# Batch 1's statistics ahead of the filters and mixing matrices, and raw matrices through two buffers

## The chip, the cores and the metric

The kernel runs on one core of a Trainium2 chip. The metric is the device time of one execution in microseconds (us), median of several executions. The engines are PE (matmul), DVE (vector), ACT (scalar), POOL (GpSimd) and SP (SyncE, which here only issues DMAs).

## What is computed

Two layers over an input of 2 batches x 128 channels x 64 x 64 positions, so 4096 tokens of 128 values a batch.

```python
x = conv_attention(x)                 # group norm, 4-head attention with rotary positions, residual
t = to_tokens(x)                      # (2, 4096, 128)
n = layernorm(t)
t = t + softmax(n @ n.T) @ n          # attention of the second layer, no projections
u = layernorm(t)
# four branches i on the first T / 2**i tokens; y_hard picks one of them
#   U+, U- = causal convolutions of u (and of u with alternating signs) with 16 filters phi
#   s_i = sum_k sigma_k**0.25 * (U+_k @ Mphi_plus[i, k] + U-_k @ Mphi_minus[i, k]) + 3 taps with M_u[i]
t = t + sum_i weight_i * pad(s_i)
```

The parts that matter here: the layer norm of the tokens ahead of the second layer's attention (batch 1's above all), and the 16 mixing matrices, which are the weighted sums over the four branches of `M_phi_plus[:, k]` and `M_phi_minus[:, k]`, times sigma_k to the power 0.25, stored as their sum and their difference.

## The kernel before

The program has four stages: the first layer's attention for both batches (up to about 1030 us), the second layer's attention for batch 0 and then for batch 1 (`attend`, up to about 1850 us), and the filter stage (the rest). All of it is unrolled Python that issues instructions one after the other. The framework then orders each engine's instructions: an instruction that is ready sooner may go ahead of one that was issued earlier, among ready ones the earlier issued goes first, and buffers of one tag are handed on as they come free. `tc.keep_in_program_order` pins an instruction behind the instruction that was issued just before it on its engine. It is used on the first `bn_stats` of each four (L692) and on the normalisation (L708).

`attend(b, p, beside, ...)` (L876) treats the 4096 x 4096 scores in quarters of 512 tokens: for j in 0 to 7, i from j to 7, so 36 blocks (j, i), since the scores are symmetric. In each block PE makes the scores (L890), ACT their exponentials (L899), PE transposes them (L906), ACT and DVE split the transposed ones into two parts (L908, L909), DVE splits the untransposed ones (L947, L948), and PE multiplies both with the tokens (L916). `close(j)` (L924) divides and adds to the tokens, with transposes on PE at L935, and calls `closed(j)`. PSUM banks for transposes come from `bank(...)`, two buffers of one tag for all users.

Other work runs beside the attention as a generator, `beside`: `next(beside, None)` is called twice a block between the scores (L975) and twice around the sums (L978, L979); in the first block only the first two are. What is left when the blocks are done is run to its end (L983).

For batch 0, `beside` is the chain in L1084:

1. `left`: what the first layer still has to do (one division and the projection of the last quarter, L333 to L364). It completes the tokens of batch 1.
2. `filters` (L792): loads phi, four small matmuls, copies into a table tile `tb`, two stores.
3. `matrices` (L846): branch weights, the tap matrices `mu`, the coefficients, and then for each of 16 k: two loads into the tile `raw` (L865, L866: 128 x 4 x 2 x 128 floats, 512 KB), a step of the generator, a weighted sum over the four branches on DVE (L716, L718), sum and difference written back into `raw` (L871, L872), and a store to `mx` in DRAM (L873). `raw` has a single buffer, so load k + 1 waits for store k.
4. `normalise(1, ...)` (L742): the statistics of batch 1 (`LayerStats.steps`, L699: eight steps of four `bn_stats` L690 and `bn_aggr` L693, and the reciprocal root, L88 on DVE and L89 on POOL), then for each quarter i the normalised tokens `y` (L709), their split into `hi` and `lo`, their transposes through a bank (L757), and the split of those (L758, L761). Quarter i waits until `closed(i)` has been called, since it overwrites what batch 0's attention reads.

The tag `raw` is also used by `tb` and `mu_raw`. The tag `low` (one buffer) holds batch 0's low parts on their way from DRAM: `ready(i)` (L1066) loads and casts quarter i + 1 at the start of block (0, i), so the last of them is asked for at block (0, 6). The stored matrices `mx` are first read in the second attention (L1097), the filter tables in the filter stage.

Of the kernel before, what the change touches and what calls it, by code (L numbers as in the profile page):

```python
# [12 lines left out]
F32 = mybir.dt.float32  # L13
# [9 lines left out]
P = 128  # L23
B, C, HH, WW = 2, 128, 64, 64
# [10 lines left out]
NK = 16  # L35
NU = 3
NBR = 4
# [26 lines left out]
def conv_attn_hybrid(ctx: ExitStack, tc: tile.TileContext, io):  # L64
    nc = tc.nc
# [25 lines left out]
    def pool(stack, name, bufs=1, **kw):  # L91
        return stack.enter_context(tc.tile_pool(name=name, bufs=bufs, reuse_waits="tile", **kw))
# [5 lines left out]
    def chain(*parts):  # L98
        for p in parts:
            yield from p  # L100
# [613 lines left out]
    def weighted_sum(dst, src, w):  # L714

        nc.vector.tensor_scalar(dst, src[:, 0], w[:, 0:1], None, ALU.mult)  # L716
        for i in range(1, NBR):
            nc.vector.scalar_tensor_tensor(dst, src[:, i], w[:, i : i + 1], dst, ALU.mult, ALU.add)  # L718
# [5 lines left out]
    def layers(st, layer0):  # L724
# [3 lines left out]
        tok = [tokens[b].tile([P, NI, C], F32, tag="t", name=f"tok{b}") for b in range(B)]  # L728
        px = pool(st, "px", side="right")
        right0, right1 = (st.enter_context(ExitStack()) for _ in range(2))  # L730
        last = pool(right0, "last", 2, side="right")
# [6 lines left out]
        def first_parts():  # L738
            hiT.append(px.tile([P, L], F32R, tag="a", name="hiT"))
            hi.append(Columns([px.tile([P, HALF], F32R, tag=f"b{n}", name=f"hi{n}") for n in range(2)]))  # L740

        def normalise(b, p, stage, gate=None):  # L742

            stats = LayerStats(p, tok[b], f"a{b}")
            yield from stats.steps()
            for i in range(NQ):
                while gate is not None and gate[0] <= i:
                    yield
                cols = bass.ts(i, 512)
                y = stage(i, 0)  # L750
                for t in range(4):
                    stats.normed(y[:, bass.ts(t, P)], 4 * i + t)
                nc.vector.tensor_copy(hi[0][:, cols], y)
                yield
                pt = side[0](f"yT{b}_{i}")
                for t in range(4):
                    nc.tensor.transpose(pt[:, bass.ts(t, P)], y[:, bass.ts(t, P)], ident)  # L757
                nc.vector.tensor_copy(hiT[0][:, cols], pt)  # L758
                low = (stage(i, 1), stage(i, 0)) if b == 0 else (loT[0][:, cols], lo[0][:, cols])
                for n, (src, first) in enumerate(((pt, hiT[0][:, cols]), (y, hi[0][:, cols]))):  # L760
                    nc.vector.tensor_tensor(low[n], src, first, ALU.subtract)  # L761
                    if b == 0:
                        nc.sync.dma_start(lows[i, n], low[n])
                yield

        def beside_last(stage):
            first_parts()
            stages = [stage(n) for n in range(2)]
            yield from normalise(0, last, lambda i, n: stages[n][:, i])


        left = layer0(tok, px, last, side, beside_last)
        psum, bank = banks(psum_a)
        side[0] = bank
# [7 lines left out]
        def transform(p):  # L782

            fw = p.tile([P, 4, NF], F32, name="fw", bufs=1)
            nc.sync.dma_start(fw, io["fw"])
            return fw
# [5 lines left out]
        def filters(p, fw):  # L792
            phi = p.tile([P, 2, TROW], F32, tag="phi", name="phi")
            nc.sync.dma_start(phi, io["phi"])
            yield
            for s in range(2):
                tb = p.tile([P, 2, 2 * TROW], F32, tag="raw", name=f"tb{s}")
                tbr = tb.rearrange("w i (o c k) -> w i c o k", c=2, k=NK)
                for c in range(2):
                    ph = bank(f"ph{s}_{c}")[:, :TROW]  # L800
                    nc.tensor.matmul(ph, fw[:, c, :], phi[:, s, :], start=True, stop=True)
                    ph = ph.rearrange("w (o k) -> w o k", k=NK)
                    nc.vector.tensor_copy(tbr[:, 0, c], ph)
                    if c == 0:
                        nc.vector.tensor_copy(tbr[:, 1, 1], ph)
                    else:
                        nc.vector.tensor_scalar(tbr[:, 1, 0], ph, -1.0, None, ALU.mult)
                    yield
                nc.sync.dma_start(tables[:, s], tb)
# [36 lines left out]
        def matrices(p):  # L846
            wbr = branch_weights(p)
            mu_raw = p.tile([P, NBR, NU, C], F32, tag="raw", name="mu_raw")
            nc.scalar.dma_start(mu_raw, io["mu"].rearrange("i n d e -> d i n e"))
            weighted_sum(mu, mu_raw, wbr)  # L850
            nc.sync.dma_start(gw, io["gw"])
            nc.vector.tensor_tensor(gw, gw, mask.unsqueeze(1).to_broadcast([P, 2, P]), ALU.mult)

            sig = p.tile([P, NK], F32, name="sig")
            nc.gpsimd.dma_start(sig, io["sigma"].partition_broadcast(P))
            quarter = p.tile([P, NK], F32, name="quarter")
            nc.gpsimd.memset(quarter, 0.25)
            nc.gpsimd.tensor_tensor(sig, sig, quarter, ALU.pow)
            coef = p.tile([P, NK, NBR], F32, name="coef")
            for k in range(NK):  # L860
                nc.vector.tensor_scalar(coef[:, k, :], wbr, sig[:, k : k + 1], None, ALU.mult)
            yield
            for k in range(NK):
                raw = p.tile([P, NBR, 2, C], F32, tag="raw", name=f"raw{k}")
                nc.sync.dma_start(raw[:, :, 0, :], io["mpp"][:, k].rearrange("i d e -> d i e"))  # L865
                nc.sync.dma_start(raw[:, :, 1, :], io["mpm"][:, k].rearrange("i d e -> d i e"))  # L866
                yield
                pm = p.tile([P, 2, C], F32, tag="pm", name=f"pm{k}")
                weighted_sum(pm, raw, coef[:, k, :])
                own = raw[:, 0]  # L870
                nc.vector.tensor_tensor(own[:, 0, :], pm[:, 0, :], pm[:, 1, :], ALU.add)  # L871
                nc.vector.tensor_tensor(own[:, 1, :], pm[:, 0, :], pm[:, 1, :], ALU.subtract)  # L872
                nc.sync.dma_start(mx[k], own)  # L873
                yield

        def attend(b, p, beside, closed, ready=lambda i: None):  # L876
# [181 lines left out]
        with ExitStack() as l1:  # L1058
            p1 = pool(l1, "l1")
            lo.append(p1.tile([P, L], F32R, name="lo"))  # L1060
            fw = transform(p1)
            with ExitStack() as part:
                p = pool(part, "l1_a")
                gate = [0]

                def ready(i):  # L1066
                    for n in range(2) if i == 0 else [i + 1]:
                        if n < NQ:
                            low = p.tile([P, 2, 512], F32, tag="low", name=f"low{n}")
                            nc.sync.dma_start(low, lows[n].rearrange("n p c -> p n c"))  # L1070
                            nc.vector.tensor_copy(loT[0][:, bass.ts(n, 512)], low[:, 0])
                            nc.vector.tensor_copy(lo[0][:, bass.ts(n, 512)], low[:, 1])

                def closed(j):
                    gate[0] = j + 1

                y = [None]

                def stage(i, n):
                    y[0] = p.tile([P, 512], F32, tag="y", name=f"y1_{i}")  # L1080
                    return y[0]

                steps = normalise(1, p1, stage, gate)
                attend(0, p1, chain(left, filters(p, fw), matrices(p), steps), closed, ready)  # L1084
            right0.close()

            mxr, mxl = (x[0].rearrange("p (k s c) -> p k s c", k=NK, s=2) for x in (hiT, loT))
            with ExitStack() as part:
                p = pool(part, "l1_b", 2)
                fed = LayerStats(ffw, tok[1], "f1")  # L1090

                def closed(j):
                    fed.take(range(4 * j, 4 * j + 4))
                    fed.close(range(4 * j, 4 * j + 4))
                    own = slice(2 * j, 2 * j + 2)
                    m = p.tile([P, 2, 2, C], F32, tag="m", name=f"m{j}")
                    nc.sync.dma_start(m, mx[own].rearrange("k p s c -> p k s c"))  # L1097
                    nc.vector.tensor_copy(mxr[:, own], m)
                    nc.vector.tensor_tensor(mxl[:, own], m, mxr[:, own], ALU.subtract)

                attend(1, p1, feed(0, p, bank, fw), closed)
# [165 lines left out]
        fw = transform(late_pool)  # L1267
        beside = chain([None] * WC, feed(1, late_pool, one_bank, fw, fed))
        steps = 0
# [153 lines left out]
```

## Time and profile before

| | us |
|---|---|
| median of 3 runs (2992.15 to 2994.43) | 2992.23 |
| the profiled execution | 2991.11 |
| its span in the profile | 2989.3 |
| PE busy, of the span | 2862.9 (96%) |
| DVE busy | 1738.8 (58%) |
| ACT busy | 1835.8 (61%) |
| POOL busy | 665.1 (22%) |

Times in the profile count from the start of the span. A line of the timeline has start, duration, engine, line of the source, operation, written tile <- read tiles, shape, count, and in brackets the idle time before it with what ended it. "SPq" is SyncE's queue issuing a DMA. Durations of consecutive DVE instructions overlap a little, so starts tell more than sums. A matmul of 512 columns shows 0.39 us but starts every 0.23 us.

### The profile page before, as it was taken

The page shows a single profiled execution, that of the slowest core. Times are in us where ns is not written, and L with a number is a line of the kernel's source. Part 1 is how long each engine was busy: PE and PEld are TensorE (multiplying, and loading weights), DVE is VectorE, ACT ScalarE, POOL GpSimd, SP SyncE. Part 2 cuts the span into 40 slices and gives each one's busy share as a digit, 9 for nine tenths or more (in the row PEclk, how much of TensorE's full clock was granted, in tenths as well). Part 3 has the DMA queues.
Part 4 walks back from the last instruction along what each step waited for, and adds up shares of the span by engine and source line. Part 5 has one row for each costly group of instructions (what it writes and reads, how often), then busy time and mean ns, then how long its engine had stood idle before and what let it go on. Part 6 is the DMA issues. An engine that isn't in the chain of part 4 may idle for free. (4 is left out here: it accounts for less than half of the span.)

```text
span 2989.3 us, 40111 instructions
## 1 busy us (share of the span) xinstructions
PE 2862.9 (96%) x13872; PEld 1822.1 (61%) x13872; DVE 1738.8 (58%) x3060; ACT 1835.8 (61%) x2363; POOL 665.1 (22%) x1328
## 2 busy tenths in 40 slices
PE   5999999999999999399999999999999999999997
PEld 2555555555455578288677786666666666666665
DVE  5364662364252389578866777555555555556553
ACT  4999999999999844144444454444444444444542
POOL 4031130021000000100101102433444444444440
PEclk9999999999999999699999999999999999999999
DMA  5021120021010132200011001333343334333331
GB/s 147 26 82 48 54 70 4 20 71 38 5 43 24 39 99 65 62 1 1 15 36 44 12 22 50 91 96 100 83 87 84 83 79 114 80 84 82 81 83 49
DMA packets 165777, 175.91 MB, mean 59 GB/s; under 512 B 45264, under 2 KB 109536, under 8 KB 165568
## 3 DMA queue, kind: packets, MB, share of 16 engines
q1 hardware_dynamic: 121760, 136.00, 16.4%
q0 software_dynamic: 40816, 34.04, 5.4%
q10 hardware_dynamic: 2992, 3.22, 0.3%
q8 instruction: 115, 1.88, 0.3%
q14 instruction: 94, 0.77, 0.1%
HBM read 130.68 MB, written 25.49 MB: 52 GB/s over the span
## 5 line engine op out<-in xcount | busy, mean ns | idle before, releaser
L433 ACT ACTIVATE e<-s 128x1536 f16<-128x1536 f32 (+1 forms) x704 | 936.7, 1428 | 35.9 <-PE s L190 31.0
L1174 DVE TENSOR_TENSOR xl<-cv,xh 128x1024 fp32r<-128x1024 f32 x512 | 603.0, 1219 | 436.5 <-ACT xh L1173 350.0
L1173 ACT CAST xh<-cv 128x1024 fp32r<-128x1024 f32 x512 | 494.7, 1018 | 523.6 <-PE cv L1164 511.8
L1139 POOL DMA_DIRECT2D tokens_in<-rows x1024 | 490.5, 487 | 680.5 <-PE cv L1164 577.1
L190 PE MATMUL s<-qs,ks 128*128 128x512 f16 x2048 | 557.5, 379 | 8.5 <-ACT e L433 3.4
L190 PE MATMUL acc<-e,v 128*97 128x512 f16 x2048 | 557.3, 379 | 3.4 <-DVE accs L389 0.2
L1196 PE MATMUL m<-xh,loT 128*128 128x512 f32 x1024 | 409.8, 400 | 0.0
L1196 PE MATMUL m<-xh,hiT 128*128 128x512 f32 x1024 | 403.2, 394 | 0.0
L190 PEld LDWEIGHTS <-v 128*97 128x97 bf16 x2048 | 254.6, 124 | 214.5 <-issue 12.5
L899 ACT ACTIVATE ey<-y,nshift 128x512 f32<-128x512 f32 x288 | 196.1, 690 | 302.1 <-PE y L890 214.8
L190 PEld LDWEIGHTS <-ks 128*128 128x128 f16 x2048 | 200.5, 99 | 227.6 <-issue 42.3
L1164 PE MATMUL cv<-tables_in,tokens_in 32*128 32x512 f32 x2048 | 300.0, 645 | 1.4 <-DVE xl L1174 1.2
L1196 PE MATMUL m<-xl,hiT 128*128 128x512 f32 x1024 | 292.3, 417 | 1.2 <-DVE xl L1174 0.5
L1196 PEld LDWEIGHTS m<-xl,hiT 128*128 128x128 f32 x1024 | 178.8, 189 | 175.8 <-issue 104.7
L1196 PEld LDWEIGHTS m<-xh,loT 128*128 128x128 f32 x1024 | 192.7, 188 | 90.7 <-issue 47.8
L1196 PEld LDWEIGHTS m<-xh,hiT 128*128 128x128 f32 x1024 | 192.4, 188 | 42.2
L916 PE MATMUL oacc<-ep,hi 128*128 128x512 f32 x576 | 209.4, 410 | 2.7 <-DVE ep L948 1.8
L909 DVE TENSOR_TENSOR eT<-eT,eT 128x512 fp32r<-128x512 f32 x224 | 146.0, 684 | 109.4 <-ACT eT L908 108.9
L389 DVE COPY accs<-acc 97x512 f32<-97x512 f32 x64 | 44.2, 690 | 275.2 <-PE acc L190 275.1
L948 DVE TENSOR_TENSOR ep<-ey,ep 128x512 fp32r<-128x512 f32 x288 | 191.9, 683 | 5.4 <-PE oacc L916 0.4
L908 ACT ACTIVATE eT<-eT 128x512 fp32r<-128x512 f32 x224 | 133.0, 607 | 94.6 <-PE eT L906 93.9
L916 PE MATMUL oacc<-eT,hi 128*128 128x512 f32 x448 | 155.7, 409 | 3.3 <-DVE oT L956 2.3
(191 smaller groups left out, 3024.0 us busy)
## 6 DMA issues: line engine op xcount, KB each, us to landing
tables_in<-tables SPq DMA_DIRECT2D x1024, 64.0 KB, 3.4
tab<-in_rot SPq DMA_DIRECT2D x32, 512.0 KB, 4.1
tokens_in<-rows POOLq DMA_DIRECT2D x1024, 16.0 KB, 3.2
qs<-term POOLq DMA_DIRECT2D x128, 64.0 KB, 2.2
rows<-uh SPq DMA_DIRECT2D x64, 128.0 KB, 1.9
ks<-term POOLq DMA_DIRECT2D x96, 64.0 KB, 1.9
accs<-back SPq DMA_DIRECT2D x32, 128.0 KB, 2.3
lows<-stage SPq DMA_DIRECT2D x16, 256.0 KB, 2.0
```

Source lines behind the costliest of these rows:

```text
L190: tc.keep_in_program_order(nc.tensor.matmul(*args, **kw))
L433: nc.scalar.activation(e[:, own, :], ps[:, own, :], AF.Exp, scale=SCORE_SCALE)
L899: nc.scalar.activation(e[:, 2 * h + q, :], ps[:, q, :], AF.Exp, bias=nshift, accum_out=den[:, t, i : i + 1])
L908: nc.scalar.activation(eT[0], pt, AF.Copy, accum_out=den[:, 4 * i + u, j : j + 1])
L909: nc.vector.tensor_tensor(eT[1], pt, eT[0], ALU.subtract)
L916: nc.tensor.matmul(acc, a[0][:, own], c, start=(start and t == 0 and n == 0), stop=(stop and t == len(es) - 1 and n == 2),)
L948: nc.vector.tensor_tensor(es[t][1], e[:, t, :], es[t][0], ALU.subtract)
L1139: nc.gpsimd.dma_start(ut[part, :, :], rows[b][ci, row : row + BP, w0 : w0 + WC // 2, :])
L1164: nc.tensor.matmul(pu[:, h, :], ut[grp, w % 2, :], tt[grp, w % 2, :], start=True, stop=True)
L1173: nc.scalar.copy(hi, pu.rearrange("d h (c k) -> d k h c", k=NK))
L1174: nc.vector.tensor_tensor(seconds[n % 2][:, :, w, 64 * g2 : 64 * g2 + 64].rearrange("d k (h c) -> d k h c", h=2), pu.rearrange("d h (c k) ...
L1196: nc.tensor.matmul(acc, m, x, start=(s == 0 and w == 0 and i == 0), stop=(s == 1 and w == WC - 1 and i == len(products) - 1),)
```

## The change

Three edits. The statistics object of batch 1 is made outside `normalise` and its steps run right behind `left`, ahead of the filters and the matrices. The raw matrices alternate between the tags `raw` (even k) and `low` (odd k, free by then). And loads 0 and 1 are issued together before the first matrix, and load k + 2 one step after matrix k is stored. For batch 0 the same statistics are made at the same place as before, only written out at the call.

```diff
-        def normalise(b, p, stage, gate=None):
-
-            stats = LayerStats(p, tok[b], f"a{b}")
-            yield from stats.steps()
+        def normalise(b, stats, stage, gate=None):
+
+
             for i in range(NQ):
...
             stages = [stage(n) for n in range(2)]
-            yield from normalise(0, last, lambda i, n: stages[n][:, i])
+            stats = LayerStats(last, tok[0], "a0")
+            yield from stats.steps()
+            yield from normalise(0, stats, lambda i, n: stages[n][:, i])
...
             yield
+            raws = {}
+
+            def load(k):
+                if k < NK:
+                    raws[k] = p.tile([P, NBR, 2, C], F32, tag="low" if k % 2 else "raw", name=f"raw{k}")
+                    nc.sync.dma_start(raws[k][:, :, 0, :], io["mpp"][:, k].rearrange("i d e -> d i e"))
+                    nc.sync.dma_start(raws[k][:, :, 1, :], io["mpm"][:, k].rearrange("i d e -> d i e"))
+
+            load(0)
+            load(1)
+            yield
             for k in range(NK):
-                raw = p.tile([P, NBR, 2, C], F32, tag="raw", name=f"raw{k}")
-                nc.sync.dma_start(raw[:, :, 0, :], io["mpp"][:, k].rearrange("i d e -> d i e"))
-                nc.sync.dma_start(raw[:, :, 1, :], io["mpm"][:, k].rearrange("i d e -> d i e"))
-                yield
+                raw = raws[k]
                 pm = p.tile([P, 2, C], F32, tag="pm", name=f"pm{k}")
                 weighted_sum(pm, raw, coef[:, k, :])
                 own = raw[:, 0]
                 nc.vector.tensor_tensor(own[:, 0, :], pm[:, 0, :], pm[:, 1, :], ALU.add)
                 nc.vector.tensor_tensor(own[:, 1, :], pm[:, 0, :], pm[:, 1, :], ALU.subtract)
                 nc.sync.dma_start(mx[k], own)
+                yield
+                load(k + 2)
                 yield
...
-                steps = normalise(1, p1, stage, gate)
-                attend(0, p1, chain(left, filters(p, fw), matrices(p), steps), closed, ready)
+                stats = LayerStats(p1, tok[1], "a1")
+                steps = chain(left, stats.steps(), filters(p, fw), matrices(p), normalise(1, stats, stage, gate))
+                attend(0, p1, steps, closed, ready)
```

## The prediction

> **What bounds the kernel now.** I read the page's 40 slices first, for a hole in the busiest engine.
>
> ```profile
> PE   5999999999999999399999999999999999999997
> DVE  5364662364252389578866777555555555556553
> PEclk9999999999999999699999999999999999999999
> ```
>
> PE is full everywhere but in slice 17 (74.7 us each, so about 1195 to 1270 us), and there the granted clock drops too. The busy time by stretch then places the hole (columns: length, PE, PE loads, DVE, ACT, POOL, each with its count, clock, DMA share, GB/s).
>
> ```profile
> 1036.00:1208.00 172.00, 169.64 (x822) 136.08 (x822) 153.78 (x351) 81.95 (x248) 3.02 (x2) 0.98 0.27 84
> 1208.00:1264.00 56.00, 6.98 (x23) 4.23 (x24) 29.04 (x124) 0.69 (x2) 8.29 (x9) 0.52 0.22 67
> 1280.00:1300.00 20.00, 20.00 (x104) 16.49 (x103) 13.49 (x27) 9.27 (x29) 0.00 (x0) 1.00 0.01 2
> ```
>
> From 1036 to 1208 us PE is 98.6% busy and DVE 89%. From 1208 to 1264 PE issues 23 matmuls, and half of DVE is idle. In the clean attention stretch (third line) DVE needs only 67%. PE's waits and its own timeline name the culprit.
>
> ```profile
> PE yT L757 <- DVE lmva L693: 47.9, 2, 40.4
> ```
>
> ```profile
> 1207.58 0.40 PE L890 MATMUL y<-hiT,loT 128*128 128x512 f32 x1
> 1248.42 0.45 PE L757 MATMUL yT<-ident,y 128*128 128x128 f32 x1 [40.45 <-DVE lmva L693]
> 1248.66 0.63 PE L935 MATMUL o<-ident,fin 128*128 128x128 f32 x2
> ```
>
> PE stands at the transpose of batch 1's first normalised quarter (L757), which needs y, which needs the statistics. Attention work (L935, whose input was ready at 1196) queues behind it. Now DVE's timeline in that hole:
>
> ```profile
> 1212.52 0.28 DVE L872 TENSOR_TENSOR raw<-pm 128x128 f32<-128x128 f32 x1
> 1218.44 0.35 DVE L716 TENSOR_SCALAR pm<-raw,coef 128x256 f32<-128x256 f32 x1 [5.63 <-DMA raw<-in_mpm]
> ...
> 1245.01 0.28 DVE L872 TENSOR_TENSOR raw<-pm 128x128 f32<-128x128 f32 x1
> 1245.21 0.48 DVE L690 BATCH_NORM_STATS2 lsta<-tok 128x6 f32<-128x128 f32 x2
> ```
>
> DVE works off the last five mixing matrices, waiting 5.6 us for each load, and starts the statistics 0.2 us after the last of them. SyncE's queue shows why each load is late: one buffer.
>
> ```profile
> 1212.83 0.34 SPq L873 DMA_DIRECT2D mx<-raw  x1
> 1214.56 0.37 SPq L865 DMA_DIRECT2D raw<-in_mpp  x1
> 1214.97 0.51 SPq L866 DMA_DIRECT2D raw<-in_mpm  x1
> 1220.90 0.34 SPq L873 DMA_DIRECT2D mx<-raw  x1
> ```
>
> Store, 1.73 us until it has landed, load, 3.9 us until DVE may start (1214.56 to 1218.44), 2.4 us of DVE: 8.1 us for each k, all in series. While attention runs beside it, DVE's part takes some 4 us instead and a turn is about 10 us (issues at 1128.5, 1138.1, 1147.7).
>
> **What the skill says.** "PSUM — Partial Sum Buffer", section "Engine vs sequencer instructions": the Vector queue is strictly first in, first out and matmuls start in program order. The trace agrees: ready transposes (L935) stood 40.4 us behind L757. "DMA: Bandwidth & Descriptors", section "Two DMAs through the same engine are not ordered": only the completion semaphore orders them, so the issuer waits for it. That is the 1.73 us from store to load. The same page's "Rules for kernel authors" says to issue a load early and wait late; the 5.6 us waits are what happens otherwise. "TensorE: Matmul & The Clock Gate", Part 1: the array's clock halves when idle and comes back after about 3.4 us busy. Here the clock was 0.52 in the hole.
>
> **Order in the code.** One step of the side generator is taken four times in each block (j, i) of the attention, twice in the first. The rest of `left` takes 11 steps: the last division 7 (its wait is 5), the projection 4. Before: filters begin at step 12, matrix k is computed at step 19 + 2k, so the last at step 49, statistics at step 50, first y at step 59. Block n holds steps 4n - 1 to 4n + 2, so steps 49 and 50 are the last two of block 12 and only matmuls lie between them: the statistics, pinned behind DVE's previous instruction, are pinned behind the last matrix. After: statistics at steps 12 to 19, filters from 21, loads 0 and 1 at 27, matrix k at 28 + 2k (the last at 58), first y at 60. Between 58 and 60 lie L909's of block 15, so y is pinned behind attention work and not behind a matrix.
>
> **The change part by part**
>
> Statistics moved. 32 L690, 32 L693, 8 L88 on DVE. The first four tiles ran from 1245.21 to about 1246.8, 1.56 us, so 8 x 1.56 = 12.5 us if alone; mixed with other work a pair advanced DVE by about 0.28 us (two L690 at 1249.89 free the engine at 1250.27, then L693 takes 0.08), hence 32 x 0.28 + 0.5 = 9.5 us. They now fall into blocks 3 to 5, about 1082 to 1105 us. Eight POOL powers (L89, 1.0 us each) move past POOL's small loads and its power of sigma, which in the trace ran at 1030 to 1038. If those queue behind them, the coefficients come at about 1105 instead, still before the first matrix: nothing. POOL was busy 3.0 of 172 us, which is the cover.
>
> Filters moved. The same instructions 9 steps later, 2.25 blocks of about 11 us, 24 us. In the trace the chain from the first filter copy (1068.3) to the first matrix (1100.8) is 32 us of copies, two table stores, and the mu load. The first matrix should so come at about 1125, block 7, where its step is. Nothing on PE reads the tables or matrices before the second attention, past 1450 us: no cost.
>
> Two buffers. Issues stay 32 loads and 16 stores on SyncE's queue. Load k + 2 still waits for store k (1.7 us), with store k + 1 and load k + 3 queued behind it; two chains of about 10 us alternate, so 5 us for each k, 16 in 80 us, done at about 1205 to 1210 if DVE keeps up. Load 1 waits for the last `low` quarter to be cast (1089.5 in the trace; its load is traced at block 6, load 1 at block 7), so it waits for nothing then. Two loads together moved at 512 KB in 3.9 us, under 5: DMA isn't the bound.
>
> The stall removed. 56.0 us from 1208 to 1264 hold 21 transposes (0.13 us each at full rate: eight take 1.04) and 2 products (0.23): 3.2 us. So 52.8 us to gain.
>
> What is late next: DVE. Before block 15 it must now do what lay in the hole: statistics 9.5 and five matrices. A matrix mixed with attention takes DVE 1.9 us (1142.17 to 1145.89 less what lies between: 0.26 + 3 x 0.40 + 2 x 0.20), alone 2.4. So 9.5 + 9.5 = 19.0 us, at most 12.5 + 12 = 24.5, into 172 - 153.8 = 18.2 us of idle. Of that idle 12.0 was waits of attention work for ACT or PE (the waits to 1208: 6.5, 3.7, 1.8), which ready side work can fill, or not. Excess: 0.8 us with all filled, 24.5 - 6.2 = 18.3 us at worst; below nothing is excluded, as DVE work is only added there. In a block of 10.2 us (L954 from 1150.57 to 1160.73) attention needs 0.67 x 10.2 = 6.8 and two matrices 3.7: 10.5, just over. I take 5 us. After block 15 DVE is at 67 to 82%, so nothing is left behind.
>
> Normalising quarters 0 and 1 lay in the hole too, about 3.2 us of DVE each. In the open, PE waits for little of it: 0 to 3 us, I take 1.
>
> Sum against the profiled execution: 2991.1 us (span 2989.3 and 1.8 around it) - 52.8 + 5 + 1 = 2944.3. The median shown is 1.1 above that execution: **2945 us**.
>
> **Rivals**
> - DVE becomes the bound (15%). For: it was 98% busy from 1190 to 1208. Against: PE lost nothing there. With the worst sums, 18.3 + 3, and up to 10 us of y waiting behind matrices in the DVE queue: about 2962.
> - The change doesn't do what it says, and the stall stays (7%): y is queued behind the last matrix all the same and a turn takes 7.5 us, as loads and DVE get in each other's way. Then that matrix ends at 1125 + 16 x 7.5 = 1245 as now, and only PE's second wait (7.45, the rest of the 47.9) and a little of the slow clock go, some 10 us: 2982. Against: y is no longer pinned to a matrix, and 512 KB take 3.9 us.
> - Slower (3%). DVE's order assumes a matrix landed sooner than it lands, and each of 16 holds DVE, with attention behind it, for the whole 3.9 us from issue: 62 us lost for 52.8 gained, with the 5 us above 3006. It decides from a mean wait of (52.8 - 6)/16 = 2.9 us. Against: up to 1208 L716 waited 1.4 us in all, for 11 matrices with one buffer.
> - More than hoped (5%): no DVE excess and the attention's own small waits (PE lost 2.4 us to 1208) go too: 2936.
>
> **Numbers.** Forecast case (2937 to 2957) 70%, the others as given. The range, 2937 to 2965, holds the first and two thirds of the DVE case: 80%. Within 0.2% (6 us, about what can be told from no change) I put 2 of the stall rival's 7%: faster 95, same 2, slower 3.
>
> **What will show it.** Right: no wait of PE for lmva; L690 at about 1082 to 1105; matrix loads in overlapping pairs, starting at about 1125 and 5 us apart; DVE over 95% in blocks 7 to 14; the clock unbroken. Wrong: L757 again with a wait of tens of us, or waits of L716 for raw above 2 us each while attention runs.

## The result and the profile after

The median is 2946.4 us (2943.7 to 2948.6, four executions) against 2992.2 before (2988.7 to 2994.4, four). The ratio is 0.985, with a 95% interval of 0.983 to 0.987: 45.8 us less, or 1.5%. The forecast was 2945 in a range of 2937 to 2965. The profiled execution took 2948.6 us, with a span of 2946.7.

First the slices of the changed kernel (73.7 us each).

```profile
PE   5999999999999999999999999999999999999997
DVE  5264563265243289878866777555555555556553
PEclk9999999999999999999999999999999999999999
```

The hole in slice 17 is closed, and the clock is unbroken. By stretch (length, PE, PE loads, DVE, ACT, POOL, clock, DMA share, GB/s):

```profile
1208.00:1264.00 56.00, 54.20 (x277) 43.83 (x276) 45.59 (x96) 25.84 (x80) 0.00 (x0) 1.00 0.04 13
1125.00:1225.00 100.00, 91.42 (x442) 69.80 (x441) 95.42 (x234) 43.30 (x129) 0.10 (x1) 1.00 0.35 105
```

Where PE had issued 23 matmuls it now issues 277. The second line is the price: while the matrices run, DVE is 95% busy and PE 91%. PE's waits from 1028 to 1470 us (total, times, longest):

```profile
PE y L901 <- DVE loT L1082: 5.7, 1, 5.7
PE eT L917 <- DVE eT L920: 3.3, 6, 1.2
PE oacc L927 <- DVE ep L959: 3.2, 9, 0.6
...
PE yT L756 <- DVE y L709: 0.3, 1, 0.3
```

The 47.9 us for the statistics (`lmva` holds the means and variances) are gone; the transposes of y (now L756) wait 0.3 us. The first line is no new wait: it stands at 1041, where PE waits for the low parts of batch 0's first tokens (`loT`), and the kernel before had it too:

```profile
PE y L890 <- DVE loT L1071: 5.5, 1, 5.5
```

New are the small waits for DVE's part of attention in the other lines. DVE's own timeline where y is made:

```profile
1198.27 0.35 DVE L716 TENSOR_SCALAR pm<-raw,coef 128x256 f32<-128x256 f32 x1
1198.66 0.69 DVE L920 TENSOR_TENSOR eT<-eT,eT 128x512 fp32r<-128x512 f32 x1
1199.26 0.47 DVE L718 SCALAR_TENSOR_TENSOR pm<-raw,coef,pm 128x256 f32<-128x256 f32 x1
1199.66 0.34 DVE L709 TENSOR_SCALAR y<-tok,lmva,lrsa 128x128 f32<-128x128 f32 x1
...
1201.22 0.28 DVE L880 TENSOR_TENSOR raw<-pm 128x128 f32<-128x128 f32 x1
```

y (L709) goes between the instructions of a matrix, and one more matrix follows later. Nothing holds it behind the last one. SyncE's queue shows two interleaved chains:

```profile
1156.92 0.34 SPq L882 DMA_DIRECT2D mx<-raw  x1
1158.82 0.37 SPq L869 DMA_DIRECT2D raw<-in_mpp  x1
...
1162.41 0.34 SPq L882 DMA_DIRECT2D mx<-raw  x1
1164.13 0.37 SPq L869 DMA_DIRECT2D raw<-in_mpp  x1
...
1167.00 0.34 SPq L882 DMA_DIRECT2D mx<-raw  x1
```

A store still precedes the load into its buffer by 1.7 to 1.9 us, but stores now come 5 us apart instead of 8 to 10.

One caution on comparing traces. The first layer, which no kernel here touches, ended at different times in the profiled executions (the table's first column). So I compare the stage: from the load of fw, which opens the second layer, to the first store of transformed tokens (rows<-uh), which is in the second attention. Before, then after:

```profile
1028.75 0.35 SPq L785 DMA_DIRECT2D fw<-in_fw  x1
...
1473.98 0.36 SPq L1022 DMA_DIRECT2D rows<-uh  x1
```

```profile
1032.97 0.35 SPq L786 DMA_DIRECT2D fw<-in_fw  x1
...
1430.73 0.36 SPq L1033 DMA_DIRECT2D rows<-uh  x1
```

445.2 us became 397.8: 47.4 us less. That is all of the difference; the spans differ by 42.6, as the second layer began 4.2 us later in this trace. From there to the first filter matmul it is 359.3 us in both, and from that to the end 1156.0 and 1156.6.

### The profile page after: what moved, and what is told of

It is laid out like the page before. It is cut to its first block, busy times and chain, and to the rows that moved or that the text cites. A ratio compares the mean times of both kernels' runs of the same rounds, so it can differ in the third digit from the quotient of the medians.

```text
span 2946.7 us, 40080 instructions
## 1 busy us (share of the span) xinstructions
PE 2861.9 (97%) x13872; PEld 1817.3 (62%) x13872; DVE 1735.2 (59%) x3060; ACT 1837.3 (62%) x2363; POOL 667.5 (23%) x1328
## 5 line engine op out<-in xcount | busy, mean ns | idle before, releaser
L920 DVE TENSOR_TENSOR eT<-eT,eT 128x512 fp32r<-128x512 f32 x224 | 147.1, 684 | 99.2 <-ACT eT L919 98.4
```

Source lines behind the costliest of these rows:

```text
L920: nc.vector.tensor_tensor(eT[1], pt, eT[0], ALU.subtract)
```

## The experiments

**Theory:** PE stood because the statistics were pinned behind the last matrix, and the matrices were late; what the new kernel pays is DVE's excess. **Rivals:** the second buffer is the cure; plain place in the order is the cause; the price isn't DVE's. All in one table, by the stage defined above (from one trace each) and the median. Of each edit only the lines that matter are shown.

| kernel | fw loaded at, us | stage, us | median, us | ratio to before (95%) |
|---|---|---|---|---|
| before | 1028.8 | 445.2 | 2992.2 | |
| after | 1033.0 | 397.8 | 2946.4 | 0.985 (0.983 to 0.987) |
| after, run again | 1030.2 | 396.2 | 2945.0 | 0.986 (0.984 to 0.987) |
| statistics first, one buffer | 1031.9 | 390.6 | 2938.3 | 0.982 (0.980 to 0.983) |
| two buffers, statistics in the old place | 1031.5 | 414.1 | 2961.6 | 0.989 (0.988 to 0.991) |
| the same, as halves of one tile | 1029.5 | 403.1 | 2952.3 | 0.988 (0.986 to 0.990) |
| one empty step | 1030.8 | 401.2 | 2950.4 | 0.986 (0.984 to 0.987) |
| matrices and y in turn | 1030.7 | 385.3 | 2936.8 | 0.981 (0.980 to 0.983) |
| weighted sums twice | 1030.8 | 414.3 | 2961.8 | 0.991 (0.989 to 0.992) |
| statistics behind matrix 11 | 1036.1 | 411.3 | 2964.3 | 0.991 (0.990 to 0.993) |

The run again, sums twice, halves and matrix 11 ran together on another occasion than the rest; before took 2989.5 there. The two traces of the changed kernel differ by 1.6 us in the stage, so a difference of less than about 2 us between two stages is not read as an effect. The expectation of the run again:

> The changed kernel unchanged, on the same chip as the other three, to compare them with: 2946 us (2943 to 2949).

### Statistics first, with one buffer

```diff
 # the changed kernel, with matrices() as it was before
-                    raws[k] = p.tile([P, NBR, 2, C], F32, tag="low" if k % 2 else "raw", name=f"raw{k}")
+                raw = p.tile([P, NBR, 2, C], F32, tag="raw", name=f"raw{k}")
```

> Statistics ahead of filters and matrices, but the raw matrices through one buffer as before. Pin theory (PE stood still because the statistics were pinned behind the last matrix, so freeing them is enough): PE's wait for lmva is gone, the sixteen matrices go on at about 10 us each until about 1285 us beside attention, DVE is not overfilled, and the 6 us that the changed kernel still loses are not lost: 2940 us (2937 to 2944). Buffer theory (the slow serial loads were the cause, and the second buffer is what cures it): y still comes after the last matrix, at 1245 us or later: 2975 to 3005 us. If the 6 us left are not DVE's excess but something else: 2946 us.

2938.3 us, in the pin theory's range. All matrices and all statistics of this kernel (durations least/median/greatest in ns, then first and last start):

```profile
L716 DVE TENSOR_SCALAR pm<-raw,coef x16: 344/354/359, 1125.8 to 1276.2; 128x256 f32<-128x256 f32 x16
```

```profile
L690 DVE BATCH_NORM_STATS2 lsta<-tok x32: 257/276/286, 1069.8 to 1088.7; 128x6 f32<-128x128 f32 x32
```

The matrices are as slow as ever, (1276.2 - 1125.8)/15 = 10.0 us a turn, and the last begins 33 us later (1276.2 against 1242.9) than in the kernel before. PE does not mind. The buffer theory falls, and so does the worth of the second buffer once the statistics are free: without it the kernel is faster by 5.6 to 7.2 us in the stage.

### Two buffers alone

```diff
 # the kernel before, with the changed matrices(), but no empty steps behind the last matrix
                 yield
-                load(k + 2)
-                yield
+                if k + 1 < NK:
+                    load(k + 2)
+                    yield
```

> Two buffers and loads ahead, but the statistics at their old place, still traced directly behind the last matrix. Pin theory with turns of 5 us: sixteen matrices from about 1100 us end at about 1180 to 1190, the statistics follow at once and are through by about 1200, before PE comes to the first transposes of y: the long stall is gone here too, with the same excess of DVE: 2946 us (2940 to 2955). If the statistics must be freed for the stall to go: 2975 us or more.

2961.6 us: neither. The pin did what was expected, as the last matrix began at 1187.9 and the statistics followed at 1192.6. But a new hole opened near 1110:

```profile
PE y L901 <- DVE loT L1082: 7.6, 1, 7.6
```

```profile
1060.77 0.36 SPq L1081 DMA_DIRECT2D low<-lows  x1
1065.24 0.37 SPq L868 DMA_DIRECT2D raw<-in_mpp  x1
...
1109.20 0.50 SPq L881 DMA_DIRECT2D mx<-raw  x1
1112.44 0.37 SPq L1081 DMA_DIRECT2D low<-lows  x1
```

Here load 1 falls on step 18, in block 4, ahead of the last two `low` quarters (asked for in blocks 5 and 6). The odd matrix took the buffer at 1065 and gave it back only when stored, at 1109; the attention's quarter came at 1112 where it had come by 1074 before. So the parts of the change depend on each other: by the count of steps, it is the nine steps of statistics in front that carry load 1 past block 6. To test whether the shared buffer made the hole, both buffers became halves of one tile of the tag `raw`:

```diff
+            both = p.tile([P, 2, NBR, 2, C], F32, tag="raw", name="both")
-                    raws[k] = p.tile([P, NBR, 2, C], F32, tag="low" if k % 2 else "raw", name=f"raw{k}")
+                    raws[k] = both[:, k % 2]
```

> Two buffers alone again, statistics pinned behind the last matrix as before, but both buffers are halves of one tile of the tag raw, so that the last two low quarters don't share a buffer with odd matrices. If the 15 us that the earlier kernel with two buffers alone lost against the changed one came from that sharing (PE stood 7.6 and 5.3 us for low quarters that waited for odd matrices), and a turn of 5 us cures the pin: 2946 us (2940 to 2952). If two buffers alone can't do it: 2958 us or more.

2952.3 us, a hair above the range; the stage is 11.0 us shorter than with the shared tag. The wait for `low` near 1110 is gone, as is the long stall: two buffers alone do cure the pin, since the last matrix now starts at 1180.3. Of the two waits in the expectation only the 7.6 us came from the sharing; the 5.3 us is the wait at the start of the stage, which every kernel has (5.2 to 5.7 us).

The stage stays 5.3 us longer than the changed kernel's, and 6.9 longer than that of its run again. Against the run again, 24 matmuls are missing in the first 113 us (520 against 544, from 7 us behind the load of fw), and 11 in the next 75 us (318 against 329), which hold the statistics (1184.3 to 1201.0) and y. At 5.05 matmuls a us (worked out below) the 35 are 6.9 us. So only a third was lost where statistics and y meet; why the rest was lost earlier is not shown.

### One empty step

```diff
             stats = LayerStats(p, tok[b], f"a{b}")
+            if b == 1:
+                yield
             yield from stats.steps()
```

> The kernel before with a single empty step of the generator between the last matrix and the statistics; nothing else. Pin theory: an attention instruction is now the one traced before the statistics, they are pinned behind that, pass the waiting matrices, and the stall is gone: 2940 to 2946 us. Theory that plain place in the order decides (statistics come later in the program than sixteen slow matrices, and DVE is in order): unchanged, 2992 us.

2950.4 us: 42 us from one line, though 4 us above the range.

```profile
L690 DVE BATCH_NORM_STATS2 lsta<-tok x32: 254/272/286, 1171.0 to 1197.1; 128x6 f32<-128x128 f32 x32
```

```profile
L716 DVE TENSOR_SCALAR pm<-raw,coef x16: 342/348/354, 1103.3 to 1254.6; 128x256 f32<-128x256 f32 x16
```

The statistics are through 57 us ahead of the last matrix, which was issued before them. So plain place in the order is not the cause: the pin was, with a single attention instruction missing between. The excess over the range lies where statistics and y come together just ahead of PE: from 1185 to 1225 PE stood 7.6 of 40 us, in the changed kernel 4.3.

### Statistics behind matrix 11

```diff
             for k in range(NK):
+                if k == 12:
+                    yield from stats.steps()
                 raw = p.tile([P, NBR, 2, C], F32, tag="raw", name=f"raw{k}")
```

> The kernel before with the statistics issued behind matrix 11 instead of behind matrix 15, pinned to it in the same way, one buffer. If each matrix that is still open when PE arrives costs one serial turn of 8.1 us, four fewer take 32.4 us off: 2960 us (2953 to 2966), with a first wait of PE of about 8 us. If the wait has to do with the statistics' or the transposes' own cost, little changes: 2985 us or more.

2964.3 us, in the range; the stage lost 33.9 us where four turns of 8.1 make 32.4. The medians agree less well: against 2989.5 on the same occasion the gain is 25.1 us. In this trace the second layer began 7.4 us later than in that of before, a delay that had arisen in the first 100 us (see the end); whether the other executions had it is not known.

```profile
PE yT L759 <- DVE y L709: 10.8, 2, 10.5
PE yT L759 <- DVE lmva L693: 8.1, 1, 8.1
```

The first wait is the 8 us expected. The second, 10.5 us for quarter 1, was 7.4 us in the kernel before. In both DVE works off the other quarters' statistics meanwhile, and here matrix 12 among them. So not all of the hole was matrices.

### Matrices and y in turn

```diff
-                steps = chain(left, stats.steps(), filters(p, fw), matrices(p), normalise(1, stats, stage, gate))
+                turns = in_turn(matrices(p), normalise(1, stats, stage, gate))
+                steps = chain(left, stats.steps(), filters(p, fw), turns)
```

`in_turn` is a new helper that takes one step of each of its generators alternately.

> The changed kernel, but from the matrices on the generator takes a step of the matrices and a step of the normalisation in turn, so one matrix a block instead of two. If DVE's excess in blocks 7 to 14 (6.8 us of attention and 3.7 of two matrices in a block of 10.2) is what the changed kernel still loses, it goes: 8.7 us a block, 2940 us (2937 to 2944), and PE is full from 1125 to 1225. If not: 2946 us.

2936.8 us, just under the range and the fastest of all. The same 100 us as above, in this kernel:

```profile
1125.00:1225.00 100.00, 98.39 (x499) 79.78 (x498) 98.21 (x227) 49.39 (x149) 0.00 (x0) 1.00 0.25 74
```

PE makes 499 matmuls where the changed kernel made 442, with DVE even busier (98%). So a full DVE alone does not slow PE; what did was two matrices a block, which ask more of DVE than a block holds.

### Weighted sums twice

```diff
                 weighted_sum(pm, raw, coef[:, k, :])
+                weighted_sum(pm, raw, coef[:, k, :])
```

> The changed kernel with every matrix's weighted sum done twice on DVE (the second writes the same values over the first): 16 x (0.26 + 3 x 0.40) = 23.4 us more DVE work, nothing more to load. If DVE is full in blocks 7 to 14 and PE pays for its excess there, nearly all of it shows: 2967 us (2960 to 2972). If the pace of the matrices is set by their loads and DVE has room between them, little shows: 2946 to 2950 us.

2961.8 us, in the range of the DVE theory at its lower end: for 23.4 us of work the stage grew by 16.5 us, or 18.1 against the run again on the same occasion. But the place is another than the theory said. This kernel, then the run again:

```profile
1125.00:1200.00 75.00, 70.62 (x341) 53.68 (x339) 74.59 (x182) 35.48 (x104) 0.00 (x0) 1.00 0.25 76
1200.00:1250.00 50.00, 40.60 (x152) 27.33 (x151) 47.84 (x122) 14.43 (x42) 0.10 (x1) 0.83 0.25 75
```

```profile
1125.00:1200.00 75.00, 69.48 (x339) 53.38 (x338) 72.38 (x181) 33.71 (x100) 0.10 (x1) 1.00 0.42 125
1200.00:1250.00 50.00, 47.19 (x236) 37.64 (x237) 42.67 (x90) 23.52 (x72) 0.00 (x0) 1.00 0.04 13
```

Up to 1200 PE makes as many matmuls as without the edit (341 and 339): DVE has no room, and it is the matrices that slow down, with stores about 8 us apart (1131.8, 1139.7, 1147.7). They run until 1250, and so into the making of y. There 152 matmuls stand against 236, a loss of 16.6 us at 5.05 a us: DVE is 96% busy, PE waits for y and for attention's parts, and the granted clock falls to 0.83. So DVE's excess does cost PE time, but the added part is paid where y is made and not in the blocks of the matrices. Where the other 5 to 7 us of the added work went is not shown.

## Why the prediction was right

- **The bound and the cause.** Right: the wait of L757, the pin, and the serial loads. The empty step shows the pin by itself, matrix 11 agrees with 8.1 us for each matrix (33.9 us of the stage for four).
- **The stall removed, 52.8 us.** Right in size. The stage lost 47.4 us, and by the counts in the next point it lost 6.3 us again to DVE's excess: together 53.7. For statistics first, 54.6 us less the 2.0 that it won there leave 52.6.
- **DVE's excess, 5 us.** Right as a difference, and its cause is shown: with the matrices in turn it goes, and with the sums doubled it grows. But the 5 was a choice within 0.8 to 18.3, so that it came so close is partly luck, and it came out of a wrong base. The prediction took it that PE lost 2.4 us from 1036 to 1208, by its busy share. A matmul shows 0.39 us but can start every 0.23, so a slower pace looks busy. Counts tell: over 172 us from about 7 us behind the load of fw, before made 822 matmuls, after 790, statistics first 832, in turn 843. A clean stretch (1300 to 1440 before) makes 707 in 140 us, 5.05 each us. After lost 32/5.05 = 6.3 us against before (its run again, with 798, 4.8); in turn won 4.2 on top of the stall, statistics first 2.0. These are estimates, since transposes and products count alike. At that rate 172 us hold some 869, so before itself was probably slowed by several us more than its busy share showed, and the rival "more than hoped" (2936) named a gain that was there, but not in this kernel. Two sums of the rivals are slightly off: 2936 should be 2937 with the 1.1 us up to the median, and the 2962 of a DVE bound leaves out the "up to 10 us of y" that it names.
- **Where things land.** Matrices from 1127 to 1208, 5.0 us a turn (predicted 1125, 1205 to 1210, 5). L716 waited 2.8 us in all for loads. Statistics at 1070.9 to 1091, not 1082 to 1105. The steps were counted right and turned into times wrongly: in the kernel before, the filters' first matmul, one step behind step 12, ran at 1067.2, and with the 4.2 us by which the second layer began later here, step 12 falls near 1070. Without cost, as they are only wanted early.
- **Load 1 waits for nothing.** Right in effect, not to the letter. SyncE's queue came to it at 1086.9, ahead of its step, and issued it at 1096.1, when the last `low` quarter had just been cast. Nothing was late by that, since load 0 came only at 1123.4. Two buffers alone, with the load nine steps earlier, show what its place was worth.
- **What the prediction did not see.** It treated both parts as needed. Each removes the long stall alone (two buffers that share `low` bring another wait in its place), and the faster pace of the two buffers accounts for most of what DVE's excess costs: with one buffer the stage is 5.6 to 7.2 us shorter. The rival "stall stays" reckoned with y behind slow matrices; statistics first with one buffer has the slow matrices, and y simply passes them.

Left open: whether removing the pins altogether does the same as the empty step. It was not tried.

## What to carry to other kernels

Ask of an instruction that holds up the busiest engine what it is ordered behind, not only what it needs: a pin to a slow chain makes that chain critical. Work that nobody waits for need not be hurried: here matrices at 10 us a turn, or one a block, cost PE less than at 5 us, because the faster pace heaped them onto an engine that attention already needed. And before a buffer is lent to another user, compare the step at which it is taken with the last step at which its owner asks for it.

## What the runs showed beside

PE's busy share hides a slower pace: 91.4 of 100 us busy with 442 matmuls, against 98.4 with 499. The time at which the second layer starts differed by some 7 us (1028.8 to 1036.1) between profiled executions of kernels with the same first layer, so single traces are better compared by stage than by span. The two latest starts (1036.1 with the statistics behind matrix 11, and 1033.0) go with the lowest clock granted from 40 to 100 us: 0.79 and 0.85, against 0.91 or 0.92 in the other eight traces. Why that clock differed is not known.
